# A hand-planned graph network stack: other planner costs, three joined slots in ten, and a last softmax in two chains

## The chip, the cores and the metric

The kernel runs on one core of a Trainium2 chip. The time is the device time of one execution in microseconds (us). The core has four compute engines that work side by side, each through its own instructions in a fixed order: PE (TensorE, matrix products), DVE (VectorE), ACT (ScalarE) and POOL (GpSimd). SP issues transfers. An instruction that needs the result of another engine waits for it, and everything behind it on its engine waits too.

## The reference

64 graphs of N = 256 nodes with D = 128 features pass four layers, each behind a layer norm and a ReLU, with a residual sum. Layers 0 to 2 are a gated recurrent graph layer of 5 steps, a Chebyshev layer and a normalised graph layer: products with a 256x256 adjacency matrix and with 128x128 weights. Layer 3 is graph attention, and most of the time goes there:

```python
def _L3_gnn_ref(x, W, b_lin, a, bias):
    s1 = jnp.einsum('bkf,ef->bke', x, W1)
    s2 = jnp.einsum('bkf,ef->bke', x, W2)
    pre = s1[:, :, None, :] + s2[:, None, :, :] + b_lin
    h = jnp.where(pre >= 0, pre, ALPHA * pre)
    e = jnp.einsum('bije,e->bij', h, a) + bias
    attn = jax.nn.softmax(e, axis=2)
    out = jax.nn.sigmoid(jnp.einsum('bij,bjf->bif', attn, x))
```

For every pair of nodes (i, j) of every graph, 256 features e of s1[i] + s2[j] go through a leaky ReLU and are summed with the weights a. That is 64 x 256 x 256 x 256 elements, which no product can replace because the nonlinearity stands inside the sum over e.

## The kernel before

**Blocks, slots and tiles.** The graphs are taken two at a time (32 pairs, `NB = 2`). The nonlinear part of one pair is cut into 64 slots (`SLOTS`), 2048 in all (`NSLOT`); 32 slots are one block (a unit of `UNITS`), 128 rows i of both graphs. A slot covers 4 rows i of both graphs against all 256 j. The 256 features stand as two halves of 128 partitions. A tile `rl` is one half of one slot: 128 partitions x 2048 numbers (1 MB), with the minimum of s1 and -s2, or the ReLU of their sum, for each of them. There are 14 tiles.

**Who makes a tile** (`work_on_tile`). DVE makes a tile of the first half in one instruction (L951, its second operand in PSUM). ACT makes one of the second half in 8 activations (L959), planned in two parts. POOL makes either in 8 instructions (L965), planned in four parts. A tile is then summed over its features by PE with a weight window `win` or `win_n` (`score`, L1039): four products, one to each 32-row group of a PSUM bank, which collects the scores of the whole block.

**Joined slots.** For the slots of `JOINED`, here one in three of the first 1952 (`SHARE`, `ALONE = 96`), POOL makes the second half in a form that can be added to the first, and then issues a DMA that adds the one tile to the other in place (`add_pair`, L985). PE scores the sum once instead of two tiles. The adding DMA is the `rl<-rl` of the profile; every issue is an instruction of POOL.

**The fronts and the tails.** `front` takes a pair through layers 0 to 2 and prepares layer 3: a long chain of steps on PE, ACT, DVE and, in each norm, POOL. In `norm`, DVE takes statistics (L483, L484), POOL makes the inverse root (`inverse_root`, L408 and L409) and the shift (L488), and ACT applies them (L492). `tail` ends a block: DVE adds an odd feature (L834) and finds the row extreme (L840), ACT takes exponentials (L846), PE turns them (L447), ACT copies (L854), PE multiplies with the features and a column of ones (L414), DVE takes the reciprocal of the sum (L866), ACT the tanh that stands for the sigmoid (L870), DVE adds the residual (L874), and SP issues the output (L878).

**What sets the order.** All instructions are put into an order before the kernel is built, by a planner that stands in the kernel's own text. It keeps a clock for each engine. `ran(engine, us, *after)` lets an engine work for so many us, and returns the time at which others can use the result, which is the clock plus `SEEN[engine]`. At each turn the engine with the earliest clock looks through what is ready by then: steps of fronts and tails (`CHAINS`) first, then filling a bank or a sum, then tiles; on PE scores stand behind the chains. Whatever the costs say decides which engine makes which tile, and when a score is placed on PE. `in_order` then ties each engine's instructions to that order. The costs are constants: `PROJECT`, `COPY`, `TANH` and so on for one or two graphs, 2.2 for a tile of DVE, 1.43 for half of one of ACT, 0.9 for a quarter of one of POOL. For the adding DMA the plan has `ISSUE` on POOL, and its landing at the later of `ADDED` after the last landing and `LANDED` after the issue. `SLACK` is waited for before an issue.

The central lines of the plan:

```python
def ran(engine, us, *after):
    start = max(clock[engine], 0.0, *after)
    clock[engine] = start + us
    return clock[engine] + SEEN[engine]
...
    issued = ran(POOL, ISSUE, since, since_z)
    done = adding[0] = max(adding[0] + ADDED, issued + LANDED)
```

Of the kernel before, what the change touches and what calls it, by code (L numbers as in the profile page):

```python
# [8 lines left out]
F32 = mybir.dt.float32  # L9
AF = mybir.ActivationFunctionType  # L10
OP = mybir.AluOpType
# [3 lines left out]
P = 128  # L15
NB = 2
# [5 lines left out]
MOST_POSITIVE = -MOST_NEGATIVE  # L22
PE, DVE, ACT, POOL = ENGINES = (mybir.EngineType.PE, mybir.EngineType.DVE, mybir.EngineType.Activation, mybir.EngineType.Pool)
SLOTS = 64
SHARE = (1, 3)
AHEAD_OF = 2
ALONE = 96
LOW = 1
ISSUE, ADDED, LANDED, SLACK = 0.65, 5.3, 6.6, 0.3


@with_exitstack
def kernel(
# [50 lines left out]
    nc = tc.nc  # L84
# [16 lines left out]

    clock = dict.fromkeys((PE, DVE, ACT, POOL), 0.0)
    queue = [0.0]
    SEEN = {PE: 0.25, DVE: 0.14, ACT: 0.5, POOL: 0.4}

    def ran(engine, us, *after):
        start = max(clock[engine], 0.0, *after)
        clock[engine] = start + us
        return clock[engine] + SEEN[engine]

# [26 lines left out]
    def by_feature(b, nb=NB):  # L137
        return b[:, 0:nb * N].rearrange("p (b n) -> p b n", b=nb)

    def by_token(b, nb=NB):  # L140
        return b[:, 0:nb * N].rearrange("p (b c n) -> p b c n", b=nb, c=NC)
# [317 lines left out]
    def feat(name, **kw):  # L459
        return work.tile([P, NB, N], F32, name=name, **kw)  # L460

    def tok(name, **kw):
        return work.tile([P, NB, NC, D], F32, name=name, **kw)
# [5 lines left out]


    PROJECT, MIX, TURN, PRODUCT, PRODUCTS = (None, 0.44, 0.86), (None, 0.88, 1.74), (None, 0.48, 0.70), (None, 0.45, 0.88), (None, 1.33, 2.64)
    COPY, BIASED, TANH, ELEMENTS = (None, 0.32, 0.48), (None, 0.40, 0.58), (None, 0.40, 0.57), (None, 0.36, 0.61)
    NORMED, STATS, LAST = (None, 0.78, 1.55), (None, 0.50, 0.87), (None, 0.55, 1.04)

    def norm(src, since, h):

        nb = src.shape[1]
        stats = work.tile([P, nb * NC, 3], F32, name="stats", bufs=4)
        mv = work.tile([P, nb * NC, 2], F32, name="mv", bufs=4)
        s, h = rows_of(src), rows_of(h)[:, :, 0:D]  # L480
        yield DVE, since
        for k in range(0, nb * NC, 2):
            nc.vector.bn_stats(stats[:, k:k + 2, :].rearrange("p k s -> p (k s)"), s[:, k:k + 2, :].rearrange("p k d -> p d k"))  # L483
        nc.vector.tensor_reduce(mv[:, :, 0], stats[:, :, 1:2], AX.X, OP.add, negate=True)  # L484
        t = ran(DVE, STATS[nb], since) + 0.5
        yield POOL, t
        inverse_root(mv[:, :, 1], stats[:, :, 2], 1.0 / D, OP.mult, LN_EPS, OP.add)
        nc.gpsimd.tensor_mul(mv[:, :, 0], mv[:, :, 0], mv[:, :, 1])  # L488
        t = ran(POOL, 1.69, t)
        yield ACT, t  # L490
        for k in range(nb * NC):
            nc.scalar.activation(h[:, k, :], s[:, k, :], AF.Relu, bias=mv[:, k, 0:1], scale=mv[:, k, 1:2])  # L492
        return ran(ACT, NORMED[nb], t)
# [4 lines left out]
    def front(p, batches):  # L498
# [227 lines left out]
        t = ran(DVE, ELEMENTS[nb], t)  # L726
        yield POOL, t
        inverse_root(rn, rn, MOST_POSITIVE, OP.min, NORM_EPS * NORM_EPS, OP.max)
        t = ran(POOL, 1.35, t) + 0.1

        yield DVE, t, 0, lambda: p < 2 or (p - 2, NC - 1) in TAILED
        x3 = kept("x3", [NC, D])
# [90 lines left out]
    def across(u):  # L823

        return [(0, c) if READY[u]["alone"] else (c, u[1]) for c in range(NB)]

    def tail(u, pe, since):

        ops = READY[u]
        x3, h3, pe = ops["x3"], ops["h3"], [by_feature(pe[0])[:, k, :] for k in range(NB)]  # L830
        yield DVE, max(since, ops["t_lin"])
        used, lin = banks_of.pop(u)[0], ops["lin"]
        for k, (b, c) in enumerate(across(u)):
            nc.vector.scalar_tensor_tensor(pe[k], ops["s2o"][:, b, :], ops["s1o"][:, b, c:c + 1], pe[k], op0=OP.min, op1=OP.add)  # L834
        t = ran(DVE, 0.9, since, ops["t_lin"])
        yield DVE, t
        sc = feat("sc", **SHORT)
        nmx = work.tile([P, NB], F32, name="nmx")
        for k, (b, c) in enumerate(across(u)):
            nc.vector.tensor_tensor_reduce(sc[:, k, :], pe[k], lin[:, b, :], scale=-1.0, scalar=MOST_POSITIVE,  # L840
                                           op0=OP.add, op1=OP.min, accum_out=nmx[:, k:k + 1])
        t = ran(DVE, 0.8, t)
        spare.append([used, t])
        yield ACT, t
        for b in range(NB):
            nc.scalar.activation(sc[:, b, :], sc[:, b, :], AF.Exp, bias=nmx[:, b:b + 1], scale=-1.0)  # L846
        t_s = ran(ACT, 0.8, t)
        yield PE, t_s, 1
        b = take()
        to_token(b[0], sc)  # L850
        t = ran(PE, TURN[2], t_s, b[1])
        yield ACT, t
        wT = tok("wT", **SHORT)
        nc.scalar.copy(wT, by_token(b[0]))  # L854
        t = ran(ACT, COPY[2], t)
        spare.append([b[0], t])
        yield PE, t, 1
        bank = take()
        po = bank[0][:, :NB * (D + 1)].rearrange("p (b d) -> p b d", b=NB)
        for k, (b, _) in enumerate(across(u)):  # L860
            for c in range(NC):
                side_by_side(po[:, k, :], wT[:, k, c, :], h3[:, b, c, :], c == 0, c == NC - 1)
        t = ran(PE, PRODUCT[2], t, bank[1])
        yield DVE, t
        rs = work.tile([P, NB], F32, name="rs")
        nc.vector.reciprocal(rs, po[:, :, D])  # L866
        t = t_s = ran(DVE, 0.15, t)
        yield ACT, t
        for k in range(NB):
            nc.scalar.activation(po[:, k, 0:D], po[:, k, 0:D], AF.Tanh, scale=rs[:, k:k + 1])  # L870
        t = ran(ACT, 0.9, t, t_s)
        yield DVE, t
        o = work.tile([P, NB, D], F32, name="o")
        nc.vector.scalar_tensor_tensor(o, po[:, :, 0:D], 0.5, x3[:, 0] if ops["alone"] else x3[:, :, u[1], :], op0=OP.mult, op1=OP.add)  # L874
        t = ran(DVE, 0.36, t)
        spare.append([bank[0], t])
        p, k = u
        nc.sync.dma_start(out[p * NB + k].rearrange("(c p) d -> p c d", p=P) if ops["alone"] else  # L878
                          out[p * NB:(p + 1) * NB, k * P:(k + 1) * P, :].rearrange("b p d -> p b d"), o)
        TAILED.add(u)  # L880


    NSLOT = NPAIR * SLOTS
# [47 lines left out]
    def work_on_tile(e):  # L931
        if e not in begun:
            k = part_of(e)
            tiles.sort(key=lambda t: t[1])
            begun[e] = [slot(k), k, *tiles.pop(0), 0]
            following[k] += 1
            held[e] += 1
            if k < 2:
                READY[where(begun[e][0])[0]]["left"][k] -= 1
        n, k, t, free, part = begun[e]  # L940
        u, r = where(n)
        ops = READY[u]
        rows = row_of(u, ops["s1"][min(k, 1)], r)
        since = max(ops["since"][k], free)

        def other(s2, b):
            return s2[:, 0 if ops["alone"] else b, :]

        if e == DVE:
            whole = [P, 4, NB, N]  # L950
            nc.vector.tensor_tensor(t, rows.to_broadcast(whole), ops["s2a"].unsqueeze(1).to_broadcast(whole), op=OP.min)  # L951
            done = ran(DVE, 2.2, since)
            ops["bank"][0][1] = max(ops["bank"][0][1], done)
            parts = 1
        elif e == ACT:
            parts = 2
            for g in (2 * part, 2 * part + 1):
                for b in range(NB):
                    nc.scalar.activation(t[:, g, b, :], other(ops["s2b"], b), AF.Relu, bias=rows[:, g, b], scale=-1.0)  # L959
            done = ran(ACT, 1.43, since)  # L960
            ops["bank"][1][1] = max(ops["bank"][1][1], done)
        else:
            parts = 4
            for b in range(NB):
                nc.gpsimd.tensor_scalar(t[:, part, b, :], other(ops["s2n" if k else "s2c"], b), rows[:, part, b],  # L965
                                        MOST_NEGATIVE, op0=OP.min, op1=OP.max)
            done = ran(POOL, 0.9, since)
        begun[e][4] += 1
        if part + 1 == parts:
            del begun[e]  # L970
            if n in WITH:
                pairs.setdefault(n, {})[k] = done, t, e
            else:
                made.append((done, n, k, t, e))
        if k < 2 and not ops["left"][k] and ops["bank"][k] and not any(b[1] == k and where(b[0])[0] == u for b in begun.values()):
            spare.append(ops["bank"][k])
            ops["bank"][k] = None
# [45 lines left out]
    def score(tile_):  # L1023
# [20 lines left out]
            held[e] -= 1  # L1044
        scored[0] += 2 if k == 2 else 1
        if left[u] == 0:
            begin(u, tail(u, [pe, 0.0], free))


    CHAINS = {}  # L1050
# [3 lines left out]
    def begin(key, steps):  # L1054
        CHAINS[key] = [steps, next(steps), 0]
# [111 lines left out]
```

## Time and profile before

| what | value |
|---|---|
| runs (3) | 4777.55, 4779.95 and 4780.21 us, median 4779.95 |
| the profiled execution, its own time | 4800.01 us |
| its span, first to last instruction | 4798.0 us |
| granted PE clock, mean | 0.997 of full speed |
| tiles made by DVE, ACT, POOL | 1756, 1259 and 1081 |
| adding DMAs | 650, 1 MB each |
| scores on PE | 3446, of four products each |
| first tile of POOL, end of its last one | 102.7 and 4776.8 us |
| last score's end to the end of the span | about 10 us |

The profile shows one execution. A busy time is the time in which an engine had at least one instruction under way; instructions of one engine overlap, so that the distance of two starts is shorter than a duration. A group of the profile is a line of the kernel, an engine and an operation, with the tiles that it writes and reads (`out<-in`), the shapes and the count; behind the bars stand its busy time, the mean duration of one in ns, and the idle time of the engine just before it with what ended most of that. A wait reads: the engine, its instruction and line, `<-`, and what ended the wait.

### The profile page before, as it was taken

What the parts mean: (1) busy time and instruction counts of PE and PEld (TensorE: products, weight loads), DVE (VectorE), ACT (ScalarE), POOL (GpSimd) and SP (SyncE); (2) the same over time, 40 slices, a digit from 0 to 9 for tenths busy, and PEclk for the clock granted to TensorE, in tenths of its full rate; (3) what the DMA queues carried; (4) which work ended last, traced back from release to release, by engine and by line L of the source; (5) the groups of instructions that cost most, each with busy time, mean ns of one, the idle gap of its engine ahead of it and who ended that gap; (6) DMA issues with size and microseconds to landing.
All of it is one profiled execution on the core that took longest, in us unless ns stands there. A gap on an engine that the chain in (4) does not pass through costs nothing.

```text
span 4798.0 us, 132133 instructions
## 1 busy us (share of the span) xinstructions
PE 4693.5 (98%) x51191; PEld 1721.1 (36%) x51191; DVE 4609.8 (96%) x3643; ACT 4686.1 (98%) x12250; POOL 4630.9 (97%) x9801
## 2 busy tenths in 40 slices
PE   8999999999999999999999999999999999999999
PEld 4333333333333333333333333333333333333333
DVE  5999999999999999999999999999999999999998
ACT  5999999999999999999999999999999999999999
POOL 2999999999999999999999999999999999999998
PEclk9999999999999999999999999999999999999999
DMA  1777778787787787777877877878778878787730
GB/s 30 161 156 163 162 160 164 155 164 161 159 163 162 155 165 161 159 161 154 167 160 159 164 156 159 167 159 164 157 156 168 162 155 164 155 164 161 158 68 5
DMA packets 138720, 725.08 MB, mean 151 GB/s; under 512 B 15721, under 2 KB 50921, under 8 KB 54889
## 3 DMA queue, kind: packets, MB, share of 16 engines
q0 software_dynamic: 93600, 681.62, 71.0%
q1 hardware_dynamic: 43768, 35.01, 2.5%
q8 instruction: 400, 6.55, 0.5%
q14 instruction: 232, 1.89, 0.1%
q10 hardware_dynamic: 720, 0.00, 0.0%
HBM read 26.48 MB, written 8.52 MB: 7 GB/s over the span
## 4 chain that ended last, share of the span: by engine, by line
PE 41%; POOL 22%; ACT 17%; DMA 9%; DVE 7%; issue 3%; POOLq 0%; ACTq 0%; DVEq 0%
PE bank L1039 25%; POOL rl L965 18%; PE bank L414 14%; ACT rl L959 13%; DMA rl<-rl 9%; DVE rl L951 6%; POOL rl L985 2%; PE bank L447 1%; ACT h L492 1%; POOL mv L409 1%; ACT bank L619 0%; PE bank L439 0%; ACT sc L846 0%; ACT bank L606 0%; ACT bank L583 0%
## 5 line engine op out<-in xcount | busy, mean ns | idle before, releaser
L959 ACT ACTIVATE rl<-bank,s1b 128x256 f32<-128x256 f32 x10072 | 4075.5, 825 | 9.8 <-DMA rl<-rl 7.5
L951 DVE TENSOR_TENSOR rl<-s1a,bank 128x2048 f32<-128x2048 f32 x1756 | 3923.8, 2278 | 29.6 <-DMA rl<-rl 16.4
L965 POOL TENSOR_SCALAR rl<-s2n,s1b 128x256 f32<-128x256 f32 x6312 | 3112.3, 931 | 10.6 <-DMA rl<-rl 0.8
L1039 PE MATMUL bank<-rl,win_n 128*32 128x512 f32 x17496 | 2197.0, 594 | 61.6 <-DMA rl<-rl 50.2
L1039 PE MATMUL bank<-rl,win 128*32 128x512 f32 x10072 | 1353.5, 594 | 0.2 <-ACT rl L959 0.2
L965 POOL TENSOR_SCALAR rl<-s2c,s1a 128x256 f32<-128x256 f32 x2336 | 1179.6, 889 | 4.9 <-PE bank L1039 1.2
L1039 PEld LDWEIGHTS bank<-rl,win_n 128*32 128x32 f32 x17496 | 562.8, 110 | 1222.3 <-issue 908.0
L985 POOL DMA_DIRECT2D rl<-rl x650 | 780.6, 1223 | 3.3 <-issue 1.1
L1039 PEld LDWEIGHTS bank<-rl,win 128*32 128x32 f32 x10072 | 337.1, 110 | 675.4 <-issue 507.4
L414 PE MATMUL bank<-mT,wts 128*32 128x512 f32 x2480 | 327.9, 593 | 0.8 <-DVE rh L587 0.8
L414 PE MATMUL bank<-adj_t,h 128*32 128x256 f32 x4960 | 297.6, 380 | 5.2 <-ACT h L641 5.1
L414 PEld LDWEIGHTS bank<-adj_t,h 128*32 128x32 f32 x4960 | 157.1, 110 | 168.8 <-ACT h L641 39.5
L492 ACT ACTIVATE h<-x,mv 128x128 f32<-128x128 f32 x376 | 173.4, 688 | 10.8 <-POOL mv L488 10.3
L583 ACT ACTIVATE bank<-bank,gate_b 128x512 f32<-128x512 f32 (+1 forms) x165 | 159.8, 969 | 14.9 <-PE bank L414 11.6
L414 PE MATMUL bank<-mT,w 128*32 128x512 f32 x1240 | 165.1, 596 | 0.0
L414 PE MATMUL bank<-hT,wts 128*32 128x512 f32 x1240 | 164.0, 595 | 0.0
L414 PE MATMUL bank<-rh,u5t 128*32 128x512 f32 x1240 | 164.0, 592 | 0.0
L606 ACT ACTIVATE bank<-bank,gate_b 128x512 f32<-128x512 f32 (+1 forms) x165 | 150.9, 915 | 8.0 <-PE bank L414 7.8
L539 ACT COPY mT<-bank 128x512 f32<-128x512 f32 x155 | 145.9, 941 | 12.8 <-PE bank L414 12.6
L619 ACT ACTIVATE bank<-bank,gate_b 128x512 f32<-128x512 f32 x155 | 145.5, 939 | 4.8 <-PE bank L414 4.8
L414 PEld LDWEIGHTS bank<-mT,wts 128*32 128x32 f32 x2480 | 82.3, 110 | 187.1 <-issue 140.7
L409 POOL TENSOR_TENSOR mv<-mv,minus_half 128x4 f32<-128x4 f32 (+1 forms) x132 | 134.1, 1016 | 11.0
(207 smaller groups left out, 3271.9 us busy)
## 6 DMA issues: line engine op xcount, KB each, us to landing
rl<-rl POOLq DMA_DIRECT2D x650, 1024.0 KB, 8.5
rows<-row SPq DMA_DIRECT2D x31, 512.0 KB
xin<-in_x_dram SPq DMA_DIRECT2D x64, 128.0 KB
out_dram<-o SPq DMA_DIRECT2D x64, 128.0 KB
row<-quarter SPq DMA_DIRECT2D x62, 2.0 KB
rows<-row SPq DMA_DIRECT2D x2, 256.0 KB
w_raw<-in_L_gnn_w_w_dram SPq DMA_DIRECT2D x3, 128.0 KB
rl<-in_L_gnn_Theta_dram SPq DMA_DIRECT2D x1, 320.0 KB
```

The source lines that it names most:

```text
L409: nc.gpsimd.tensor_tensor(t, t, minus_half[:, 0:t.shape[1]], op=OP.pow)
L414: nc.tensor.matmul(o[g:g + 32], w[:, g:g + 32], t, start=start, stop=stop, skip_group_check=True)
L492: nc.scalar.activation(h[:, k, :], s[:, k, :], AF.Relu, bias=mv[:, k, 0:1], scale=mv[:, k, 1:2])
L539: nc.scalar.copy(c, seen(bank))
L583: nc.scalar.activation(seen(r), seen(pr), AF.Tanh, bias=br, scale=0.5)
L606: nc.scalar.activation(seen(pr), seen(pr), AF.Tanh, bias=bz, scale=0.5)
L619: nc.scalar.activation(seen(pv), seen(pv), AF.Tanh, bias=bh_n, scale=-1.0)
L951: nc.vector.tensor_tensor(t, rows.to_broadcast(whole), ops["s2a"].unsqueeze(1).to_broadcast(whole), op=OP.min)
L959: nc.scalar.activation(t[:, g, b, :], other(ops["s2b"], b), AF.Relu, bias=rows[:, g, b], scale=-1.0)
L965: nc.gpsimd.tensor_scalar(t[:, part, b, :], other(ops["s2n" if k else "s2c"], b), rows[:, part, b], MOST_NEGATIVE, op0=OP.min, op1=OP.max)
L985: nc.gpsimd.dma_start(out=t.rearrange("p g b n -> p (g b n)"), in_=z.rearrange("p g b n -> p (g b n)"), accum_op=OP.add)
L1039: nc.tensor.matmul(pe[g * 32:(g + 1) * 32, :], w[:, 31 - r:63 - r], flat(t[:, g]), start=False, stop=(left[u] == 0), skip_group_check=True)
```

## The change

Five things are different. `SHARE` goes from one joined slot in three to three in ten. The planner's costs are other numbers, for the tiles of ACT and POOL, the steps of the fronts, POOL's part of a norm, and the issue and landing of an adding DMA. `SEEN` is smaller for ACT and POOL, and in `norm` the extra time between DVE's statistics and POOL goes from 0.5 to 0.1 (after the root of layer 2 an extra 0.1 is gone). `tail` takes a list `own` of graphs; for the very last block it is begun twice, once for each graph, as two chains with one graph each. All other blocks have one tail for both. What is computed is the same.

```diff
-SHARE = (1, 3)
+SHARE = (3, 10)
...
-ISSUE, ADDED, LANDED, SLACK = 0.65, 5.3, 6.6, 0.3
+ISSUE, ADDED, LANDED, SLACK = 0.93, 5.9, 7.0, 0.3
...
-    SEEN = {PE: 0.25, DVE: 0.14, ACT: 0.5, POOL: 0.4}
+    SEEN = {PE: 0.25, DVE: 0.14, ACT: 0.2, POOL: 0.13}
...
-    COPY, BIASED, TANH, ELEMENTS = (None, 0.32, 0.48), (None, 0.40, 0.58), (None, 0.40, 0.57), (None, 0.36, 0.61)
-    NORMED, STATS, LAST = (None, 0.78, 1.55), (None, 0.50, 0.87), (None, 0.55, 1.04)
+    COPY, BIASED, TANH, ELEMENTS = (None, 0.34, 0.50), (None, 0.40, 0.59), (None, 0.41, 0.59), (None, 0.36, 0.61)
+    ODD, EXTREME, EXPS, TANHS = (None, 0.40, 0.90), (None, 0.35, 0.69), (None, 0.41, 0.82), (None, 0.45, 0.90)
+    NORMED, STATS, LAST = (None, 0.80, 1.60), (None, 0.50, 0.87), (None, 0.55, 1.04)
...
-        t = ran(DVE, STATS[nb], since) + 0.5
+        t = ran(DVE, STATS[nb], since) + 0.1
...
-        t = ran(POOL, 1.69, t)
+        t = ran(POOL, 1.78, t)
...
-        t = ran(POOL, 1.35, t) + 0.1
+        t = ran(POOL, 1.45, t)
...
-    def tail(u, pe, since):
+    def tail(u, pe, since, own=range(NB)):
...
+        nb = len(own)
+        of = [(*across(u)[k], by_feature(pe[0])[:, k, :]) for k in own]
...
-        t = ran(DVE, 0.8, t)
-        spare.append([used, t])
+        t = ran(DVE, EXTREME[nb], t)
+        if own[-1] == NB - 1:
+            spare.append([banks_of.pop(u)[0], t])
...
-            done = ran(ACT, 1.43, since)
+            done = ran(ACT, 1.46, since)
...
-            done = ran(POOL, 0.9, since)
+            done = ran(POOL, 0.873, since)
...
-            begin(u, tail(u, [pe, 0.0], free))
+            if u == UNITS[-1]:
+                for k in range(NB):
+                    begin((*u, k), tail(u, [pe, 0.0], free, [k]))
+            else:
+                begin(u, tail(u, [pe, 0.0], free))
```

Within `tail` every step runs over `of` and `nb` where it ran over both graphs, and the output is issued for the graphs of `own`.

More of the change, by code (lines that the diff above doesn't have):

```diff
@@ L825, in across @@
         return [(0, c) if READY[u]["alone"] else (c, u[1]) for c in range(NB)]
-    def tail(u, pe, since):
+    def tail(u, pe, since, own=range(NB)):
         ops = READY[u]
-        x3, h3, pe = ops["x3"], ops["h3"], [by_feature(pe[0])[:, k, :] for k in range(NB)]
+        nb = len(own)
+        of = [(*across(u)[k], by_feature(pe[0])[:, k, :]) for k in own]
+        x3, h3, lin = ops["x3"], ops["h3"], ops["lin"]
         yield DVE, max(since, ops["t_lin"])
[L832 to L835, printed above, removed]
+        for b, c, s in of:
+            nc.vector.scalar_tensor_tensor(s, ops["s2o"][:, b, :], ops["s1o"][:, b, c:c + 1], s, op0=OP.min, op1=OP.add)
+        t = ran(DVE, ODD[nb], since, ops["t_lin"])
         yield DVE, t
-        sc = feat("sc", **SHORT)
+        sc = feat("sc", **SHORT)[:, 0:nb]
         nmx = work.tile([P, NB], F32, name="nmx")
-        for k, (b, c) in enumerate(across(u)):
-            nc.vector.tensor_tensor_reduce(sc[:, k, :], pe[k], lin[:, b, :], scale=-1.0, scalar=MOST_POSITIVE,
+        for k, (b, _, s) in enumerate(of):
+            nc.vector.tensor_tensor_reduce(sc[:, k, :], s, lin[:, b, :], scale=-1.0, scalar=MOST_POSITIVE,
                                            op0=OP.add, op1=OP.min, accum_out=nmx[:, k:k + 1])
-        t = ran(DVE, 0.8, t)
-        spare.append([used, t])
+        t = ran(DVE, EXTREME[nb], t)
+        if own[-1] == NB - 1:
+            spare.append([banks_of.pop(u)[0], t])
         yield ACT, t
-        for b in range(NB):
-            nc.scalar.activation(sc[:, b, :], sc[:, b, :], AF.Exp, bias=nmx[:, b:b + 1], scale=-1.0)
-        t_s = ran(ACT, 0.8, t)
+        for k in range(nb):
+            nc.scalar.activation(sc[:, k, :], sc[:, k, :], AF.Exp, bias=nmx[:, k:k + 1], scale=-1.0)
+        t_s = ran(ACT, EXPS[nb], t)
         yield PE, t_s, 1
@@ L850, in tail @@
         to_token(b[0], sc)
-        t = ran(PE, TURN[2], t_s, b[1])
+        t = ran(PE, TURN[nb], t_s, b[1])
         yield ACT, t
-        wT = tok("wT", **SHORT)
-        nc.scalar.copy(wT, by_token(b[0]))
-        t = ran(ACT, COPY[2], t)
+        wT = tok("wT", **SHORT)[:, 0:nb]
+        nc.scalar.copy(wT, by_token(b[0], nb))
+        t = ran(ACT, COPY[nb], t)
         spare.append([b[0], t])
@@ L858, in tail @@
         bank = take()
-        po = bank[0][:, :NB * (D + 1)].rearrange("p (b d) -> p b d", b=NB)
-        for k, (b, _) in enumerate(across(u)):
+        po = bank[0][:, :nb * (D + 1)].rearrange("p (b d) -> p b d", b=nb)
+        for k, (b, _, _) in enumerate(of):
             for c in range(NC):
                 side_by_side(po[:, k, :], wT[:, k, c, :], h3[:, b, c, :], c == 0, c == NC - 1)
-        t = ran(PE, PRODUCT[2], t, bank[1])
+        t = ran(PE, PRODUCT[nb], t, bank[1])
         yield DVE, t
         rs = work.tile([P, NB], F32, name="rs")
-        nc.vector.reciprocal(rs, po[:, :, D])
+        nc.vector.reciprocal(rs[:, 0:nb], po[:, :, D])
         t = t_s = ran(DVE, 0.15, t)
         yield ACT, t
-        for k in range(NB):
+        for k in range(nb):
             nc.scalar.activation(po[:, k, 0:D], po[:, k, 0:D], AF.Tanh, scale=rs[:, k:k + 1])
-        t = ran(ACT, 0.9, t, t_s)
+        t = ran(ACT, TANHS[nb], t, t_s)
         yield DVE, t
-        o = work.tile([P, NB, D], F32, name="o")
-        nc.vector.scalar_tensor_tensor(o, po[:, :, 0:D], 0.5, x3[:, 0] if ops["alone"] else x3[:, :, u[1], :], op0=OP.mult, op1=OP.add)
+        o = work.tile([P, NB, D], F32, name="o")[:, 0:nb]
+        p, c = u
+        batches = slice(own[0], own[-1] + 1)
+        nc.vector.scalar_tensor_tensor(o, po[:, :, 0:D], 0.5, x3[:, 0] if ops["alone"] else x3[:, batches, c, :], op0=OP.mult, op1=OP.add)
         t = ran(DVE, 0.36, t)
         spare.append([bank[0], t])
[L877 to L880, printed above, removed]
+        nc.sync.dma_start(out[p * NB + c].rearrange("(c p) d -> p c d", p=P) if ops["alone"] else
+                          out[p * NB:(p + 1) * NB, c * P:(c + 1) * P, :].rearrange("b p d -> p b d")[:, batches], o)
+        if own[-1] == NB - 1:
+            TAILED.add(u)
     NSLOT = NPAIR * SLOTS
```

## The prediction

> **What bounds the kernel now.** I read the page's first part, then the waits of each engine, then the costliest groups, then the timeline of single engines to price one tile.
>
> ```profile
> PE 4693.5 (98%) x51191; PEld 1721.1 (36%) x51191; DVE 4609.8 (96%) x3643; ACT 4686.1 (98%) x12250; POOL 4630.9 (97%) x9801
> ```
>
> Four engines are within 2% of each other, so busy shares alone do not name the pacemaker. The waits of POOL do:
>
> ```profile
> POOL mv L408 <- DVE stats L483: 77.1, 7, 45.3
> POOL rn L408 <- DVE rn L725: 12.5, 2, 7.2
> POOL rl L965 <- DMA rl<-rl: 1.2, 3, 0.4
> POOL rl L965 <- PE bank L1039: 1.2, 1, 1.2
> ```
>
> The columns are total us, times, longest. The long waits of the first two rows lie before 102 us (POOL's timeline shows them at 4 to 102 us, while the first batches are prepared). From its first tile at 102.7 us to its last one, which ends at 4776.8, POOL waits some 7 us in all. No other engine is that full, by its idle times:
>
> ```profile
> L951 DVE TENSOR_TENSOR rl<-s1a,bank 128x2048 f32<-128x2048 f32 x1756 | 3923.8, 2278 | 29.6 <-DMA rl<-rl 16.4
> L1039 PE MATMUL bank<-rl,win_n 128*32 128x512 f32 x17496 | 2197.0, 594 | 61.6 <-DMA rl<-rl 50.2
> L985 POOL DMA_DIRECT2D rl<-rl x650 | 780.6, 1223 | 3.3 <-issue 1.1
> ```
>
> PE is idle 4798.0 - 4693.5 = 104.5 us, 50.2 of it for the adding DMAs that POOL issues; DVE is idle 188 us. The order on each engine is fixed beforehand, so an engine that is slower in fact than in the plan holds up the others: POOL is that engine. Its timeline shows why:
>
> ```profile
> 2599.67 1.98 POOL L985 DMA_DIRECT2D rl<-rl  x1
> 2600.29 4.95 POOL L965 TENSOR_SCALAR rl<-s2n,s1b 128x256 f32<-128x256 f32 x8
> 2603.87 2.23 POOL L985 DMA_DIRECT2D rl<-rl  x1
> 2604.49 5.19 POOL L965 TENSOR_SCALAR rl<-s2n,s1b 128x256 f32<-128x256 f32 x8
> 2608.10 5.08 POOL L965 TENSOR_SCALAR rl<-s2c,s1a 128x256 f32<-128x256 f32 x8
> 2611.67 2.36 POOL L985 DMA_DIRECT2D rl<-rl  x1
> ```
>
> Columns: start, duration, instruction. By starts a DMA issue takes 0.62 us (2599.67 to 2600.29). By ends it takes 0.86 (2605.24 to 2606.10) or 0.85, and a tile of eight instructions 3.58 or 3.50. Starts run ahead of ends (1.98, 2.23, 2.36 us of duration), and the lag is paid when the queue drains. The old plan has 0.65 for an issue, some 0.2 too little, 650 times: 130 us by which POOL runs late, less what the plan's 3.6 for a tile has too much.
>
> **The change part by part.** Counts come from the instruction orders of the two built programs.
>
> 1. *Fewer adding DMAs (SHARE 3/10).* Of the 1952 slots that may be joined, 585 instead of 650 are: 65 issues fewer on POOL, 65 x 0.85 = -55 us (bounds by starts and by the group's busy time: 0.62 gives -40, 780.6 / 650 = 1.20 gives -78; I take the ends, since ends are what others wait for). Each slot no longer joined is scored in two halves: 3511 scores instead of 3446. A score costs PE 0.86 us, the distance of two starts here, though each row says 1.04:
>
> ```profile
> 4653.41 1.04 PE L1039 MATMUL bank<-rl,win_n 128*32 128x512 f32 x8
> 4654.26 1.04 PE L1039 MATMUL bank<-rl,win 128*32 128x512 f32 x8
> ```
>
> So PE gets 65 x 0.86 = +56 us.
>
> 2. *New costs (ACT 1.46 for 1.43, POOL 0.873 for 0.9, ISSUE 0.93 for 0.65, and the front's).* They move tiles: DVE makes 1775 of them instead of 1756, ACT 1235 (9880 instructions) instead of 1259, POOL 1086 instead of 1081. Prices from undisturbed stretches:
>
> ```profile
> 4676.69 52.68 ACT L959 ACTIVATE rl<-bank,s1b 128x256 f32<-128x256 f32 x144
> 4677.14 46.23 DVE L951 TENSOR_TENSOR rl<-s1a,bank 128x2048 f32<-128x2048 f32 x21
> ```
>
> 52.68 / 144 x 8 = 2.93 for a tile of ACT, 46.23 / 21 = 2.20 for one of DVE. ACT -24 x 2.93 = -70 us, DVE +19 x 2.20 = +42, POOL +5 x 3.55 = +18. With part 1: POOL -37, ACT -70, DVE +42, PE +56. The four sum to about -9: work is not removed, it is moved off the engine that never waits, onto two that do.
>
> 3. *Later landings, earlier ends (LANDED 7.0, ADDED 5.9, SEEN).* The plan believed a sum landed 0.65 + 0.4 + 6.6 = 7.65 us after POOL got to the issue; now 0.93 + 0.13 + 7.0 = 8.06, counted from the end of POOL's last instruction instead of the next start, a lag of 0.5 us or more. The trace:
>
> ```profile
> DMA to landing us min/median/max: 6.8/8.5/14.6
> ```
>
> So the old plan is 0.85 us early against the median and the new one about right; PE's 50.2 us of DMA waits should mostly go. Kept in full they are the other bound. The Trainium skill (DMA: Bandwidth & Descriptors, "Anatomy of one DMA — SWDGE (gpsimd) path") fits 2.0 us plus bytes / 436e3, an estimate of 4.4 us for this 1 MB and against any later landing; the trace's 8.5 decides, and by the page PE's waits would not shrink at all.
>
> A tile from ACT or POOL now counts as readable 0.2 or 0.13 us after its end, before 0.5 or 0.4 after its start slot; where the engine is ahead of the plan this costs nothing, and ACT has 70 us less to do. In the norms the extra 0.5 us between DVE's statistics and POOL becomes 0.1: POOL may now stand at L408 for DVE, with its tiles and DMAs queued behind, and ACT's L492 behind it. The trace has about 1 us of that wait after 102 us, because POOL runs late; if POOL keeps time the bound is 0.4 us x 124 = +50, at best 0. I take 0, the row's value.
>
> 4. *The last block's softmax in two chains.* The last chain:
>
> ```profile
> 4790.97 0.59 ACT L854 COPY wT<-bank 128x512 f32<-128x512 f32 x1 [0.63 <-PE bank L447]
> 4791.61 1.95 PE L414 MATMUL bank<-h,wT 128*32 128x129 f32 x32 [0.68 <-ACT wT L854]
> 4793.90 0.72 ACT L870 ACTIVATE bank<-bank,rs 128x128 f32<-128x128 f32 x2 [2.34 <-DVE rs L866]
> 4795.10 0.37 SPq L878 DMA_DIRECT2D out_dram<-o  x1
> ```
>
> Half the copy, then the product of the second batch behind that of the first, which starts some 0.6 us sooner, and one tanh instead of two (-0.35), against a second issue on SP (0.37): between -1.6 and +0.4, I take -1. It is the only part at the very end, and 0.02% of the time.
>
> **The sum.** POOL's time is the span as long as it waits for nobody: 4798 - 37 - 1 = 4760. PE's own sum: busy 4693.5 + 56 = 4749.5; with its 54.3 us of other idle time kept and the DMA waits gone, 4804. Both cannot hold; PE's other waits are partly waits for chains that a late POOL holds up, so some of them go as well. I take the middle, 4782, 16 us (0.33%) under the span of 4798.0. The profiled execution took 4800.01 us by its time, 20 more than the median of the runs, so against that median of 4779.95 the forecast is **4764 us**. DVE allows it: 4609.8 + 42 = 4652, leaving 130 us of its 188 idle.
>
> The Trainium skill (Perfetto Trace Analysis, "Identifying the Most-Contended Engine") judges TensorE by its weight loads, here 36%, and not by matmul busy time. By that rule 56 us more on PE cost nothing and the time would be POOL's sum, 4760 of span; the starts at 0.86 us without a gap speak against so much room.
>
> **The rivals.**
>
> *PE takes over, part of its waits goes.* 4804 of span, 4786 on the runs' scale: no change that can be told (0.2% of 4780 is 10 us, about what a measurement of this kernel can tell). For: PE has the least idle time of the three that are given more or equal work. Against: where PE paces, tiles lie ready and most of its waits end. 0.17.
>
> *PE takes over with its waits kept.* The place is the scoring line L1039, the price 56 us: if the landings still come late (the maximum is 14.6) and 104.5 us stay idle, the span is 4749.5 + 104.5 = 4854, the time 4836, slower by 1.2%. It decides from the point where PE's stalls fall by less than 56 - 10 = 46 us. 0.13.
>
> *POOL waits for DVE in the norms.* DVE has 42 us more and is planned to hand over 0.4 us later than POOL arrives: 4760 + 50 = 4810 of span, 4792, slower by 0.25%. For: the margin is cut from 0.5 to 0.1. Against: POOL never arrived early so far. 0.12.
>
> *The constants do less than the counts say*, because landing times scatter: gain and loss cancel within 0.2%, as in the first rival; I count it there.
>
> **How the numbers follow.** The forecast's case, 4745 to 4778, has 0.58: 0.53 for its part under 4770, which is faster by over 0.2%, and 0.05 for the part above. POOL's sum alone (4742) lies just below it. Within 0.2% is 0.21, that 0.05 and 0.16 of the first rival; slower 0.26, the second and third rivals (0.25) and 0.01 of the first. The range reaches from POOL's sum less 5 us to between the two slower rivals: 4737 to 4808. The likeliest case's own range is 4745 to 4778.
>
> **What would show it.** Right: POOL busy time down by some 40 us at 585 issues and still without waits after 105 us; PE's idle time for the adding DMA under 25 us; ACT's idle time up by 50 or more. Wrong: PE's total idle still near 100 us with the span above 4800 (second rival), or waits of POOL L408 for DVE's statistics of tens of us after 105 us (third). The last output after the last score should come about 1 us sooner than 10.1 us.

## The result and the profile after

The changed kernel takes 4721.76 us (median of 4, 4720.04 to 4723.54) against 4778.75 before: ratio 0.988, 95% interval 0.9865 to 0.9899, 57 us or 1.2% faster. The forecast was 4764, the range ended at 4737: the direction was right, the size off by more than three times.

The page's first part of the changed kernel, and its chain of work by engine:

```profile
PE 4693.0 (99%) x51711; PEld 1724.1 (37%) x51711; DVE 4638.2 (98%) x3664; ACT 4615.2 (98%) x12059; POOL 4565.5 (97%) x9776
...
PE 80%; DVE 10%; POOL 4%; issue 2%; DMA 2%; ACT 2%; SPq 0%; POOLq 0%; DVEq 0%; ACTq 0%
```

The same view of the kernel before, of the chain alone:

```profile
PE 41%; POOL 22%; ACT 17%; DMA 9%; DVE 7%; issue 3%; POOLq 0%; ACTq 0%; DVEq 0%
```

PE's share of the chain doubled, POOL's and ACT's nearly vanished: the chain ran back and forth between engines that waited for POOL and its sums; now it stays mostly on PE. That alone does not make PE the engine that sets the time (see the rivals below). The span fell from 4798.0 to 4718.2, PE's idle time from 104.5 us to 25.2, and PE is busy 4693.0 us, as long as before, with 65 scores more. The groups of the changed kernel:

```profile
L956 DVE TENSOR_TENSOR rl<-s1a,bank 128x2048 f32<-128x2048 f32 x1775 | 3964.5, 2277 | 8.7 <-DMA rl<-rl 4.9
...
L1044 PE MATMUL bank<-rl,win_n 128*32 128x512 f32 x18208 | 2258.9, 593 | 7.0 <-DMA rl<-rl 4.9
L1044 PE MATMUL bank<-rl,win 128*32 128x512 f32 x9880 | 1303.8, 593 | 0.0
...
L990 POOL DMA_DIRECT2D rl<-rl x585 | 617.4, 1068 | 3.8 <-DVE rl L956 1.5
```

PE's idle time for adding DMAs went from 50.2 us to 4.9, DVE's before its tiles from 29.6 to 8.7. POOL still waits for nobody once the fronts of the first pair are through (its first three rows lie before 96 us), as its waits show:

```profile
POOL mv L408 <- DVE stats L484: 70.0, 6, 37.1
POOL rl L970 <- ACT s1b L802: 7.5, 1, 7.5
POOL rn L408 <- DVE rn L726: 5.4, 1, 5.4
POOL rl L990 <- DVE rl L956: 1.5, 1, 1.5
```

Since POOL has no slack in either kernel, the span can be added up along POOL, by the distances of the ends of its instructions (worked out from the traces; us):

| run | span | until first tile | tiles | adding DMAs | front steps | after last tile |
|---|---|---|---|---|---|---|
| before | 4798.0 | 102.7 | 1081 x 3.591 = 3882 | 650 x 0.828 = 538 | 254 | 21.1 |
| changed | 4718.2 | 95.6 | 1086 x 3.570 = 3877 | 585 x 0.816 = 478 | 253 | 14.9 |
| changed, level of before | 4737.2 | 95.8 | 1086 x 3.586 = 3894 | 585 x 0.816 = 477 | 254 | 15.6 |

One kernel's time differs by some 20 us between batches of runs (the kernel before took 4779 beside the changed kernel and 4800 in its profiled execution), so the third row, the run a1_after, beside which the kernel before took 4798, is the fair one: -61 for the DMAs, +12 for the tiles, -7 at the beginning and -5.5 at the end. On this level PE is idle for 33.7 us and busy for 10.0 us more than before:

```profile
PE 4703.5 (99%) x51711; PEld 1729.9 (37%) x51711; DVE 4640.7 (98%) x3664; ACT 4622.2 (98%) x12059; POOL 4584.8 (97%) x9776
```

### The profile page after: what moved, and what is told of

Same layout as the page of the kernel before. It is cut to its first block, busy times and chain, and to the rows that moved or that the text cites. A ratio compares the mean times of both kernels' runs of the same rounds, so it can differ in the third digit from the quotient of the medians.

```text
span 4718.2 us, 133077 instructions
## 1 busy us (share of the span) xinstructions
PE 4693.0 (99%) x51711; PEld 1724.1 (37%) x51711; DVE 4638.2 (98%) x3664; ACT 4615.2 (98%) x12059; POOL 4565.5 (97%) x9776
## 4 chain that ended last, share of the span: by engine, by line
PE 80%; DVE 10%; POOL 4%; issue 2%; DMA 2%; ACT 2%; SPq 0%; POOLq 0%; DVEq 0%; ACTq 0%
PE bank L1044 52%; PE bank L414 25%; DVE rl L956 8%; POOL rl L970 3%; PE bank L447 2%; DMA rl<-rl 2%; ACT rl L964 1%; PE bank L439 1%; POOL rl L990 0%; DVE bank L627 0%; DVE d L623 0%; DVE hT L631 0%; DVE rh L588 0%; DVE stats L484 0%; DVE bank L836 0%
## 5 line engine op out<-in xcount | busy, mean ns | idle before, releaser
L956 DVE TENSOR_TENSOR rl<-s1a,bank 128x2048 f32<-128x2048 f32 x1775 | 3964.5, 2277 | 8.7 <-DMA rl<-rl 4.9
L964 ACT ACTIVATE rl<-bank,s1b 128x256 f32<-128x256 f32 x9880 | 3938.3, 727 | 5.2 <-PE bank L1044 3.5
L1044 PE MATMUL bank<-rl,win_n 128*32 128x512 f32 x18208 | 2258.9, 593 | 7.0 <-DMA rl<-rl 4.9
L1044 PE MATMUL bank<-rl,win 128*32 128x512 f32 x9880 | 1303.8, 593 | 0.0
L970 POOL TENSOR_SCALAR rl<-s2c,s1a 128x256 f32<-128x256 f32 x2184 | 1054.3, 741 | 2.4
L1044 PEld LDWEIGHTS bank<-rl,win_n 128*32 128x32 f32 x18208 | 586.0, 110 | 1210.5 <-issue 1022.9
L990 POOL DMA_DIRECT2D rl<-rl x585 | 617.4, 1068 | 3.8 <-DVE rl L956 1.5
L1044 PEld LDWEIGHTS bank<-rl,win 128*32 128x32 f32 x9880 | 319.9, 110 | 633.8 <-issue 509.2
L584 ACT ACTIVATE bank<-bank,gate_b 128x512 f32<-128x512 f32 (+1 forms) x165 | 138.0, 836 | 20.1 <-PE bank L414 17.4
L607 ACT ACTIVATE bank<-bank,gate_b 128x512 f32<-128x512 f32 (+1 forms) x165 | 138.4, 839 | 9.7 <-PE bank L414 9.5
L540 ACT COPY mT<-bank 128x512 f32<-128x512 f32 x155 | 123.9, 800 | 12.7 <-PE bank L414 11.9
```

What stands on the lines that cost most here:

```text
L540: nc.scalar.copy(c, seen(bank))
L584: nc.scalar.activation(seen(r), seen(pr), AF.Tanh, bias=br, scale=0.5)
L607: nc.scalar.activation(seen(pr), seen(pr), AF.Tanh, bias=bz, scale=0.5)
L990: nc.gpsimd.dma_start(out=t.rearrange("p g b n -> p (g b n)"), in_=z.rearrange("p g b n -> p (g b n)"), accum_op=OP.add)
L1044: nc.tensor.matmul(pe[g * 32:(g + 1) * 32, :], w[:, 31 - r:63 - r], flat(t[:, g]), start=False, stop=(left[u] == 0), skip_group_check=True)
```

## The experiments

All ratios are to the kernel before, run on the same chip in the same batch. Tiles are DVE / ACT / POOL.

| run | tiles | adding DMAs | ratio [95% interval] |
|---|---|---|---|
| a1_after | 1775 / 1235 / 1086 | 585 | 0.9877 [0.9861, 0.9894] |
| e1_share | 1764 / 1234 / 1098 | 585 | 1.0006 [0.9997, 1.0016] |
| e2_costs | 1781 / 1242 / 1073 | 650 | 0.9912 [0.9898, 0.9927] |
| e4_landings | 1776 / 1276 / 1044 | 650 | 0.9992 [0.9983, 1.0002] |
| e3_onetail | 1775 / 1235 / 1086 | 585 | 0.9886 [0.9872, 0.9901] |
| f1_seen | 1775 / 1235 / 1086 | 585 | 0.9887 [0.9872, 0.9902] |
| f2_oldcosts | 1774 / 1265 / 1057 | 585 | 0.9928 [0.9913, 0.9942] |
| e5_early_landing | 1775 / 1234 / 1087 | 585 | 0.9888 [0.9873, 0.9903] |
| e6_cheap_issue | 1759 / 1208 / 1129 | 585 | 1.0211 [1.0190, 1.0231] |
| e10_act | 1767 / 1245 / 1084 | 585 | 0.9901 [0.9884, 0.9917] |
| e7_share516 | 1777 / 1238 / 1081 | 610 | 0.9895 [0.9880, 0.9910] |
| e8_jitter | 1774 / 1235 / 1087 | 585 | 0.9886 [0.9871, 0.9901] |
| g5_true | 1775 / 1243 / 1078 | 585 | 0.9856 [0.9843, 0.9870] |
| g1_two | 1786 / 1260 / 1050 | 650 | 0.9917 [0.9903, 0.9930] |
| g3_split | 1758 / 1257 / 1081 | 650 | 0.9987 [0.9979, 0.9996] |
| g4_mix | 1775 / 1241 / 1080 | 585 | 0.9846 [0.9832, 0.9859] |

**The parts alone.**

```diff
 e1_share, from before
-SHARE = (1, 3)
+SHARE = (3, 10)
 e2_costs, from the changed kernel
-SHARE = (3, 10)
+SHARE = (1, 3)
 e4_landings, from before
-ISSUE, ADDED, LANDED, SLACK = 0.65, 5.3, 6.6, 0.3
+ISSUE, ADDED, LANDED, SLACK = 0.93, 5.9, 7.0, 0.3
```

> The kernel before with SHARE 3/10 alone. Theory L (the gain is POOL's load): 65 issues of 0.85 us leave POOL, the busiest engine, so the time falls by 40 to 55 us, to 4725 to 4740. Theory P (the gain is the plan's better agreement with the chip): the plan still believes an issue costs 0.65 us and a landing 7.65, PE gets 65 x 0.86 = 56 us more and keeps most of its 105 us idle; the time falls by less than 20 us or rises, 4760 to 4800.

> The changed kernel with SHARE back at 1/3; costs, landings and the last block's two chains stay. Theory L: nearly all of the gain is lost, 4765 to 4780. Theory P: most of it stays, 4715 to 4740, with PE idle for adding DMAs under 25 us; by P alone it could be even faster than the changed kernel, since PE has 56 us less to do.

> The kernel before with ISSUE 0.93, ADDED 5.9 and LANDED 7.0 alone, SHARE 1/3, old SEEN and old engine costs. Theory P, landings: PE's 50 us of idle time for adding DMAs fall under 20 and the time falls by 25 to 50 us, 4730 to 4755. Theory L: the load is the old one, within 10 us of 4779.

SHARE alone gains nothing, and theory L as I had put it falls. The tiles tell why: the old plan, which books an issue at 0.65 us, filled the freed time with 17 tiles more on POOL, 17 x 3.59 = 61 us, which eats the 65 x 0.83 = 54 us of the issues. POOL's load is the old one, and so is the time. The landings and the dearer issue alone gain nothing either, though PE's waits for adding DMAs are gone. So theory P, which gave them 25 to 50 us, falls there. Yet e2_costs, the changed kernel without its SHARE, keeps 42 us of the gain (4757.7 against 4799.3), as theory P had it. Along POOL this adds up: 8 tiles fewer than before are 29 us, its first tile comes 7 us earlier, and the end after its last one is 6 us shorter. The first part of e4_landings, its group of ACT's tiles, and POOL's waits:

```profile
PE 4735.7 (99%) x51191; PEld 1820.3 (38%) x51191; DVE 4651.9 (97%) x3663; ACT 4727.6 (99%) x12386; POOL 4505.4 (94%) x9505
```

```profile
L959 ACT ACTIVATE rl<-bank,s1b 128x256 f32<-128x256 f32 x10208 | 4320.0, 1100 | 0.4 <-PE bank L1039 0.2
```

```profile
POOL mv L408 <- DVE stats L483: 90.9, 32, 43.6
POOL rl L985 <- DVE rl L951: 39.0, 41, 2.4
```

With a dearer issue the plan took 37 tiles off POOL and gave ACT 17 more. ACT sits at 0.4 us of idle time before its tiles; POOL waits. ACT paces instead of POOL, at nearly the same time. Both theories were too simple; a third, made after these runs, fits all three: the division of the work decides, by the true load of whichever engine has the most (theory B).

**Margins, costs, landings within the changed kernel.** f1_seen puts SEEN and the 0.5 of `norm` back, e5_early_landing ADDED 5.3 and LANDED 6.6; f2_oldcosts has these old costs (and those of the fronts):

```diff
-            done = ran(ACT, 1.46, since)
+            done = ran(ACT, 1.43, since)
-            done = ran(POOL, 0.873, since)
+            done = ran(POOL, 0.9, since)
```

> The changed kernel once more, as the yardstick for the other runs of this batch. Its ratio to the kernel before was 0.9882 [0.9865, 0.9899]; expected 0.986 to 0.990 on this chip too.

> The changed kernel with the old SEEN (ACT 0.5, POOL 0.4) and the old 0.5 us between DVE's statistics and POOL. The tiles are divided as in the changed kernel (1775, 1235, 1086), so only the order differs. Theory S (the gain comes from results that count as readable earlier, which packs the chains of the fronts tighter): over half of the 1.2% is lost, ratio 0.994 or more. Theory C (it comes from the engines' costs, which make POOL and ACT keep time): within 0.003 of the changed kernel.

> The changed kernel with the old costs of ACT's and POOL's tiles, of the fronts and of POOL's part of the norms; SEEN, ISSUE, landings and SHARE stay new. The tiles are DVE 1774, ACT 1265, POOL 1057. Theory C: over half of the gain is lost, 0.994 or more. Theory S: within 0.003 of the changed kernel. By load alone POOL makes 29 tiles fewer than in the changed kernel (29 x 3.5 = 102 us less) and ACT 30 more (30 x 2.9 = 88 us more): ACT would be the busiest by far.

> The changed kernel with the old landings (ADDED 5.3, LANDED 6.6); ISSUE stays 0.93. Theory D (the gain is PE's waits for adding DMAs): those waits return to 30 to 50 us of idle time from 5, and the ratio rises by 0.005 to 0.009. Theory C or S: under 0.003, since in the changed kernel PE has tiles enough to score meanwhile.

SEEN and the landings are worth 4 and 5 us of medians in this batch, little more than the 2 to 4 us (0.0004 to 0.0009 of ratio) by which the control e8_jitter below differs from the changed kernel. The costs are worth 24 us (4763 against 4739), about two fifths of the gain and not over half: with 30 tiles more ACT paces, as in e4_landings. Theory S falls in both runs; theory C is right about f1_seen and put the costs too high in f2_oldcosts. Theory D falls: e5_early_landing has 12.6 us of waits for adding DMAs on PE, not 30 to 50; so they were due to POOL's lateness more than to the plan's landing time.

**The load, tested in the losing direction.** e6_cheap_issue puts ISSUE alone back to 0.65; e10_act has 1.43 for ACT, e7_share516 `SHARE = (5, 16)`, e8_jitter 0.612 for 0.61 in ELEMENTS.

> The changed kernel with ISSUE back at 0.65 and nothing else. The plan now gives POOL 1129 tiles beside the 585 issues (changed kernel: 1086). Theory B (the division of the work decides: the span is POOL's true load, at 3.55 us a tile and 0.85 an issue, as long as POOL has the most): POOL has 43 x 3.55 = 153 us more than in the changed kernel, whose span on this chip was 4737, so 4860 to 4890, ratio 1.013 to 1.019, slower than the kernel before. Theory O (the order on each engine and the margins decide): 0.988 to 0.994.

> The changed kernel with 1.43 for half a tile of ACT instead of 1.46. Tiles: DVE 1767, ACT 1245, POOL 1084. Theory B: ACT stalled some 74 us in the changed kernel, so it carries 10 x 2.93 = 29 us more unhurt, POOL gets 7 us less and DVE 18 less; PE stays; the time falls by 0 to 7 us, ratio 0.986 to 0.988. Theory O: the costs are less true than 1.46, so no gain or a loss, 0.988 to 0.990.

> The changed kernel with SHARE 5/16 (610 adding DMAs, between 585 and 650). PE gets 25 x 0.86 = 22 us less, POOL 25 x 0.85 - 5 x 3.55 = 3 us more. Theory B: PE (34 us idle) no longer paces, POOL does, so the time stays within 5 us of the changed kernel, ratio 0.987 to 0.989. If PE were the only bound: 0.984.

> A control: the changed kernel with 0.612 for 0.61 in ELEMENTS, a cost that is as true as before. The tiles move by one (DVE 1774, POOL 1087), the order in many places. What it differs by is the chance part of any such plan: expected within 0.0015 of the changed kernel's 0.988.

One number makes the changed kernel slower than the kernel before, a little beyond the range that theory B gave (1.0211 against 1.013 to 1.019). It costs the changed kernel what 43 tiles more on POOL cost: 43 x 3.58 = 154 us, where the profiled spans are 4892.0 in e6_cheap_issue and 4737.2 in a1_after, and the medians are 150 us apart from the control of the batch. Where the others waited in e6_cheap_issue:

```profile
ACT h L493 <- POOL mv L489: 143.3, 99, 3.2
...
DVE rl L956 <- DMA rl<-rl: 74.1, 53, 4.4
```

ACT and DVE wait for POOL's norms and sums, as theory B has it. The sweep around the changed kernel finds no gain: e10_act is 7 us slower than the control where I expected 0 to 7 us of gain, e7_share516 4 us slower, and all three lie within 0.0025 of the changed kernel's ratio. One control is too little to say how much of that is the chance part of another order.

**The division alone.** g5_true changes three numbers of the kernel before, g1_two two; g3_split has only the two last chains and the tails' own costs; g4_mix is the changed kernel with 1.45 and 0.879.

```diff
 g5_true, from before
-SHARE = (1, 3)
+SHARE = (3, 10)
-ISSUE, ADDED, LANDED, SLACK = 0.65, 5.3, 6.6, 0.3
+ISSUE, ADDED, LANDED, SLACK = 0.82, 5.3, 6.6, 0.3
-            done = ran(ACT, 1.43, since)
+            done = ran(ACT, 1.46, since)
```

> The kernel before with three numbers changed: ISSUE 0.82 (as the trace has it by ends), half a tile of ACT 1.46, SHARE 3/10. Landings, SEEN, the fronts' costs, the norms and the last block stay old. Tiles: DVE 1775, ACT 1243, POOL 1078 with 585 adding DMAs, close to the changed kernel's 1775, 1235 and 1086. Theory B (division alone): POOL 8 x 3.58 = 29 us less than in the changed kernel, ACT 8 x 2.93 = 23 us more, so as fast or up to 10 us faster: ratio 0.985 to 0.989. Theory O (part of the gain needs the truer order, landings or SEEN): 0.991 to 0.996, with PE idle for adding DMAs at 30 us or more.

> The kernel before with ISSUE 0.93 and half a tile of ACT 1.46, SHARE 1/3. Tiles: DVE 1786, ACT 1260, POOL 1050, 650 adding DMAs. POOL has 31 x 3.59 = 111 us less than before, ACT as much as before, DVE 30 x 2.2 = 66 us more. Theory B: POOL paces no more, ACT does, whose saturated run with 1276 tiles spanned 4793: 4793 - 16 x 2.93 = 4746, ratio 0.989; PE has 56 us less to do than in the changed kernel. Theory O: within 0.003 of the kernel before.

> The kernel before with the last block's two chains alone (and the tails' own costs, which move POOL by no tile and DVE by two). The end after the last score should be 2 us shorter: ratio 0.9993 to 0.9997. Over 0.003 of gain would mean that the order as a whole has shifted.

> The changed kernel with 1.45 for ACT's half tile and 0.879 for POOL's quarter. Tiles: DVE 1775, ACT 1241, POOL 1080. POOL has 6 x 3.58 = 21 us less, ACT 6 x 2.93 = 18 us more. Theory B: PE and DVE are the next bounds (PE idle 25 to 34 us), so a gain of 0 to 10 us on the changed kernel, ratio 0.985 to 0.988.

g5_true gets the whole gain (its interval overlaps that of a1_after), without a word on landings, SEEN, fronts or the last block. Its first part, and PE's scores:

```profile
PE 4687.4 (99%) x51711; PEld 1732.9 (37%) x51711; DVE 4638.6 (98%) x3662; ACT 4634.3 (98%) x12122; POOL 4550.2 (96%) x9712
```

```profile
L1039 PE MATMUL bank<-rl,win_n 128*32 128x512 f32 x18144 | 2234.6, 593 | 13.0 <-DVE rl L951 7.2 <-DMA rl<-rl 5.5
```

PE waits 5.5 us for adding DMAs, with the old landing times: theory O falls. g1_two relieves POOL and leaves ACT its 1260 tiles; ACT paces (busy 4680.1 of 4747.4 us) and two thirds of the changed kernel's gain come, somewhat less than I expected. Beside e4_landings, which has the same ISSUE but the old cost of ACT, 16 tiles fewer on ACT bring the ratio from 0.9992 to 0.9917 (the landings differ as well). g3_split is worth 0.13%, 6 us (2 to 10), where its end is 2 us shorter; the rest is not explained. e3_onetail, for which I expected a rise of 2 us, does not differ from the changed kernel beyond the intervals. g4_mix, with 6 tiles fewer on POOL and 6 more on ACT than the changed kernel, has the lowest time of the study: 0.9846, 4715.12 us against 4789.02 before in its batch; its interval overlaps that of g5_true. Its first part:

```profile
PE 4694.3 (100%) x51711; PEld 1737.5 (37%) x51711; DVE 4637.3 (98%) x3664; ACT 4632.0 (98%) x12107; POOL 4557.3 (97%) x9728
```

PE is idle 18.8 us in all.

## Why the prediction was wrong in size

*What bounds the kernel* was right: POOL is the engine without slack, and it has more to do than the plan believed. e6_cheap_issue and the table of POOL's time show it, and in the changed kernel it still is.

*Parts 1 and 2*, POOL's -37 us: on the fair level -61 + 12 = -49, and -12 at the two ends. An issue by ends costs 0.83, as priced; 538 - 477 is more than 65 x 0.85 because the remaining ones are a little shorter, 0.816. The tiles got 12 us dearer and not 18. What the sum left out is the beginning: POOL's first tile comes 7 us earlier. In the runs with the old SEEN and the old 0.5 us it comes at 100.7 (f1_seen) to 102.7 us, in those with the new ones at 91.1 (f2_oldcosts) to 99.3 (e7_share516). So the fronts' tighter chains bring it forward, but the amount varies with the order.

*The step that failed is "the middle" of the sum: POOL's sum, 4760, was averaged with "PE's own sum", 4804, on the ground that PE keeps its idle time of 54.3 us outside the DMA waits and that 65 scores more add 56 us to its busy time.* On the fair level PE kept 33.7 us of idle time in all, and its busy time rose by 10.0 us. So 71 us of idle time went, and 46 us that the busy time before had counted as work; together they paid for the 56 us of scores and for the 61 us by which the span fell. PE's busy time was not all work: a score's row lasts 1.04 us where the next starts after 0.86, so a wait of up to 0.18 us between two of them does not show as idle. e6_cheap_issue shows that both kinds of wait come with an overloaded POOL: with the same number of matmuls as a1_after, PE is busy 75 us longer and idle 113.5 us of the 4892.0.

```profile
PE 4778.5 (98%) x51711; PEld 1741.1 (36%) x51711; DVE 4619.7 (94%) x3648; ACT 4557.0 (93%) x11843; POOL 4734.6 (97%) x10120
```

Without the averaging the forecast would have been 4742 on the runs' scale, still 20 us above the result; the issues, the tiles and the two ends make up for that, as the table has them.

By the Trainium skill's rule (Perfetto Trace Analysis, "Identifying the Most-Contended Engine"), cited in the prediction and set aside, the extra scores cost nothing. The outcome agrees: the time fell to POOL's sum and below it. The share of weight loads does not rank these kernels, though: it is 36% before, where PE is idle 104.5 us, and 37% in g4_mix, where it is idle 18.8.

*Part 3*: PE's waits for adding DMAs fell under 25 us as said, to 4.9. But they are an effect: with the old landings they stay small once POOL keeps time (12.6 in e5_early_landing, 5.5 in g5_true). The cut in `norm` cost nothing, as taken: POOL has no such wait after the first pair. One sign that the prediction named did not come: ACT's idle time was to rise by 50 us or more and went from 111.9 us to 115.0 on the fair level, since the span fell nearly as much as ACT's work.

*Part 4*: the new end of the changed kernel:

```profile
4713.02 0.77 ACT L857 COPY wT<-bank 128x256 f32<-128x256 f32 x2
4713.44 1.33 PE L414 MATMUL bank<-h,wT 128*32 128x129 f32 x32
...
4715.02 0.34 ACT L873 ACTIVATE bank<-bank,rs 128x128 f32<-128x128 f32 x1 [0.25 <-DVE rs L869]
4715.22 0.83 SPq L882 DMA_DIRECT2D out_dram<-o  x2
```

The product starts before the second copy is done. From DVE's first step (4710.47) to the end are 7.7 us, before 10.0 (from 4787.92): 2.3 us, not 1. e3_onetail and the changed kernel overlap in their intervals.

*The rivals*: PE did not take over in either form. It has the least idle time, but e7_share516 takes 25 scores off it (22 us) and leaves POOL's load within 3 us, and its time is 4726.9 us beside the control's 4723.2. PE's busy time does not fall by 22 us either; the control's is 4696.5:

```profile
PE 4694.8 (99%) x51511; PEld 1735.2 (37%) x51511; DVE 4642.3 (98%) x3666; ACT 4623.2 (98%) x12083; POOL 4570.6 (97%) x9761
```

The wait of POOL for DVE in the norms grows where POOL has slack. With the margin of 0.1 us that is f2_oldcosts, where ACT paces and POOL waits anyway; whether it would cost time on a POOL that paces is not shown.

```profile
POOL mv L408 <- DVE stats L484: 101.3, 55, 37.2
```

## What to carry to other kernels

Where a plan divides work by its own costs, one wrong cost hurts through the division more than through the order (here 61 to 154 us against 4 or 5): look for the engine that never waits, price its instructions by the distance of their ends, and correct the cost that the plan has too low, together with that of the engine that would take the work over. A busy share of PE with overlapping matmuls contains small waits, so new work on PE can be free; ask first for whom PE waits. A part of a change that gains nothing alone may gain with others: SHARE did nothing, a dearer issue (0.93, with later landings) did nothing, and SHARE with an issue of 0.82 and ACT's new cost brought 1.4%. Which of the three could be left out there was tried only in part.

## What was not expected

The starts of POOL's tile instructions lie 0.450 us apart in the profile of the kernel before, and 0.448 in that of the changed one; in a1_after, the same changed kernel in another batch, 0.450 again. DVE's tiles are 2.198 in all three. 1086 tiles of 8 at 3.586 instead of 3.570 us are 17 of the 19 us between the two profiles of the changed kernel. The other profiles fit: 0.448 in e8_jitter, beside which the kernel before took 4778 us, 0.449 in g3_split, where it took 4789, and 0.450 in f1_seen, where it took 4798. The record has the same chip number for these three batches. What sets POOL's pace there was not tried.
